# Macaron block on one core: queries of the second token group and the output signs held into the attention turns, the next element's first FFN begun in the prologue, small vectors loaded behind the matrices

## The chip, the core and the metric

One core of a Trainium2 chip. The metric is the device time of one execution in microseconds (us), as the median of several runs. The engines are TensorE (PE; PEld is its weight load), VectorE (DVE), ScalarE (ACT), GpSimd (POOL) and SyncE (SP, which here only issues DMAs).

## What is computed

Two batch elements of 1024 tokens, 512 wide, fp32. Cut to what matters:

```python
def bitnet_linear(x, weight, scale):            # q (512), k (128), v (128), o (512) outputs
    s = max(mean(abs(weight), axis=1), 1e-8)
    y = (x @ sign(weight / s).T) * (s * scale)
    return nan_to_num(y, nan=0, posinf=1e6, neginf=-1e6)

def attn(x):                                    # 32 heads of 16, 8 key/value heads
    q, k, v = (bitnet_linear(x, w, sc) for w, sc in ...)
    a = softmax(q @ k.T / sqrt(16))             # every head, 1024 x 1024
    return bitnet_linear(a @ v, o_weight, o_scale)

def ffn(x):                                     # base matrix + 8 experts of rank 16, top 2
    w = top2_softmax(x @ W_router.T)
    return x @ W_base.T + b_base + 2 * sum_e(w[e] * (x @ A[e].T) @ B[e].T)

x = x + 0.5 * ffn(layernorm(x))                 # first FFN
x = x + attn(layernorm(x))
x = x + 0.5 * ffn(layernorm(x))                 # second FFN
```

## The kernel before

Tokens are taken in groups `(b, g)`: batch element `b`, group `g` of 512 tokens (four tiles of 128). `first(b, g)` is the first FFN, the second layer norm and the projections of a group. Its projections come in six parts, items 0 to 3 for the queries (each serves two key/value heads' groups), 4 for the keys, 5 for the values. A part is eight fp32r matmuls (`pq`, L541; sign matrix times high and low half of the input) or 32 small ones (`pv`), a scaled copy `y` on ACT (L546), the replacement of NaN and infinities in `finite` (`lo`, `ma`, `z` on VectorE and GpSimd), a split of the result into a high and a low half (L574 on ACT, L580), and four stores to DRAM. For element 0 the query parts that are not marked `fast` store from the ACT and the GpSimd queue (L577, L584), all others from SP. `second(b, g)` normalises the attention output, applies the output projection (`po`, L679) and runs the second FFN (names ending in `s`, as `pbs`, `phs`, where the first FFN has `pbf`, `phf`). In an FFN `pt` are transposes, `ph` the router and low-rank matmuls (L363), `hwp` transposes of the weighted low-rank part, `pb` the base matmuls in fp32 (L388 and L393), and the bias is added on GpSimd (L383).

`binarize` makes the signs and scales of a weight matrix: absolute values on ACT, their sums by fp32 matmuls with ones (`pm_k`, `pm_q`, `pm_v`, `pm_o`, L488), reciprocals `rs` on VectorE (L498), products on GpSimd (L502), signs on ACT (L506, L509).

Attention is cut into 32 units: element, half of the queries (512), key/value head. A unit takes four turns. In a turn the scores of one unit are computed for the row maxima (`m`, eight matmuls, L796, reduced by eight VectorE instructions `mn`, L804), those of the unit before for the exponentials (`e`, 16 matmuls, L831 and L835, with eight ACT instructions `es`, L838), and the exponentials are multiplied with the values (`av`, L868). The first turns have no exponentials yet (lead-in). `place` loads a unit's queries and keys from DRAM; unit 8 is the first that needs queries of token group 1 of element 0, unit 16 the first of element 1.

The order of instructions on every engine is made while the program is built. Work is written as generators (strands) that yield the engine they want next: `"P"` TensorE, `"v"` VectorE, `"a"` ACT, `"g"` GpSimd, `"d"` SP, `"u"` a condition, `"r"` a buffer, `"j"` a join. `Flow` gives places to strands by rank (a lower number goes first) and by an estimate of when a result is due. Before the loop (the prologue) `flow.play` runs the strands freely. In `attention` three written orders say where in a turn a strand may place an instruction: `F` on TensorE, `V` and `W` on VectorE, `C` and `D` on ACT. A turn is `LEAD_IN` as long as there are no exponentials, else `FULL` when a strand wants TensorE (with places `F`), else `BARE`. `need` and `until` place everything that is left until a condition holds. At most three chains of strands are alive at a time; a chain starts at the turn that stands beside it in `chains`.

In `ffn_tiles`, `early` says that the base matmuls of all tiles are begun ahead of the routing. It is `flow.free`, true in the prologue and behind the loop.

Of the kernel before, what the change touches and what calls it, by code (L numbers as in the profile page):

```python
# [12 lines left out]
ALU = mybir.AluOpType  # L13
AX = mybir.AxisListType

P = 128
# [9 lines left out]
TG = 4  # L26
# [6 lines left out]
def macaron_kernel(ctx: ExitStack, tc: tile.TileContext, x_in, wbT, b_base, wrT, aT, bT,  # L33
                   wqT, q_sc, wkT, k_sc, wvT, v_sc, woT, o_sc, out):
    nc = tc.nc
# [39 lines left out]
    bh = const.tile([P, D], F32, name="bh")  # L75
    nc.gpsimd.dma_start(bh, b_base.partition_broadcast(P))
    wraw = {}
# [11 lines left out]
    qsc = const.tile([P, KC], F32, name="qsc")  # L89
    nc.gpsimd.dma_start(qsc, q_sc)  # L90
    ksc = const.tile([P, 1], F32, name="ksc")
    nc.gpsimd.dma_start(ksc, k_sc)
    vsc = const.tile([P, P], F32, name="vsc")
    nc.gpsimd.dma_start(vsc, v_sc.partition_broadcast(P))
    osc = const.tile([P, D], F32, name="osc")
    nc.gpsimd.dma_start(osc, o_sc.partition_broadcast(P))

# [37 lines left out]
    class Flow:  # L135
        def __init__(self):
            self.t, self.free, self.after, self.strands, self.n = 0, True, False, [], 0
            self.stock = dict(m=3, n=4, t=11, xT=2, xL=2, hT=1, fb=6)
            self.lock = None
            self.busy = dict.fromkeys("Pvagd", 0)  # L140
            self.pool = 0
# [199 lines left out]
    def ffn_tiles(xt, name, rank, tiles, xT, hT, mv, given, mv2, summed, store, loads):  # L341
# [36 lines left out]
        def base(t):  # L378
            if not early:
                yield "r", dict(t=1)  # L380
            yield "u", lambda: "bias" in signs
            yield "g", ""
            nc.gpsimd.tensor_tensor(xt[:, t, :], xt[:, t, :], bh, ALU.add)  # L383
            for c in range(KC):
                yield ("P", "P") if c else ("P", "", flow.t, 1)
                if c == 0:
                    pb = bank(f"pb{n}_{t}")
                nc.tensor.matmul(pb, xT[:, c, t * P:(t + 1) * P], wb[:, c, :],  # L388
                                 start=(c == 0), stop=False)
                flow.lock = bs[t] if c < KC - 1 else None  # L390
            yield "u", lambda: ready
            yield "P", "a", ready[0]
            nc.tensor.matmul(pb, hT[0][:, t * P:(t + 1) * P], lb, start=False, stop=True)  # L393
            if flow.free:
                yield "v", "P"
                nc.vector.scalar_tensor_tensor(xt[:, t, :], pb, 0.5, xt[:, t, :], ALU.mult, ALU.add)
                flow.give(fb=1, **({} if early else dict(t=1)))
            else:
                yield "a", "P"
                hb = t512(f"hb{n}_{t}")  # L400
                nc.scalar.activation(hb, pb, AF.Copy, scale=0.5)  # L401
                flow.give(fb=1)
                yield "g", "a"
                nc.gpsimd.tensor_tensor(xt[:, t, :], xt[:, t, :], hb, ALU.add)  # L404
                if not early:
                    flow.give(t=1)
            if store is not None:
                yield ("a" if flow.free else "d"), "v" if flow.free else "g"
                (nc.scalar if flow.free else nc.sync).dma_start(store[t * P:(t + 1) * P, :],
                                                                xt[:, t, :])  # L410
            if mv2 is not None:
                yield "v", "v" if flow.free else "g"
                stats(xt, t, mv2, n)
                summed.add(t)


        bs, ready, early = {}, [], flow.free
        if early:
# [60 lines left out]
    def binarize(w, n_out, name, sc, rank, at):  # L479
# [29 lines left out]
        nc.scalar.activation(wr[:, KC - 1, :], w[:, KC - 1, :], AF.Sign)  # L509

        if name in "vo":
            yield "v", ""
            nc.vector.tensor_tensor(sc, s, sc, ALU.mult)
        else:
            yield "P", "", None, 1
            pt = bank(f"col_{name}")
            for c in range(n_out // P):
                nc.tensor.transpose(pt[:, c * P:(c + 1) * P], s[:, c * P:(c + 1) * P], ident)
            yield "v", "P"
            nc.vector.tensor_tensor(sc, sc, pt[:, 0:n_out].rearrange("p (c n) -> p c n", n=P)[:, :, 0],  # L520
                                    ALU.mult)
            flow.give(fb=1)
# [70 lines left out]

    def qkv(b, g, xs, items, ranks, fast):

        at = ("v", flow.t)
        for i, rank in zip(items, ranks):
            parts[b, g, i] = [None]
            yield "u", lambda: ("q" if i < KC else "k" if i == KC else "v") in signs
            parts[b, g, i][0] = flow.spawn(qkv_part(b, g, xs, i, fast.get(i, 0), at), rank)  # L600
# [63 lines left out]
    def o_proj(b, g, hs, rank, mv, given, fast=False):  # L664
# [39 lines left out]
        for t in range(TG):  # L704
# [14 lines left out]
            "A3 m0(3) e0(0) V e0(5) D e1(0) e0(7) e0(6) e1(5) m0(2) e1(7) V e1(6) W m0(5) m0(4)")  # L719
    LEAD_IN = ("m0(0) m0(6) m0(1) V m0(7) F C S V m0(4) m0(2) V F C m0(5) V F C V m0(3) V F C V")  # L720
    FULL, BARE, LEAD_IN = (
# [156 lines left out]

    def attention(chains, n0):

# [3 lines left out]
        flow.stock["fb"] -= 4  # L884
        live = []

# [14 lines left out]
        for n in range(n0, TU * len(units) + LEAD + 1):  # L901
            begin = flow.t = max(flow.t, begin + span)
            m, e, a = todo(n, 0), todo(n, LEAD), todo(n, LEAD + 1)
            live = [c for c in live if not c.done]
# [58 lines left out]

    def first(b, g, items, ranks, fast={}, loads=None):

# [9 lines left out]
        else:  # L975
# [5 lines left out]
              for t, c in ((tag, bufs), ("xL", 2))]  # L981
        yield "j", [flow.spawn(ln_T(xt, f"a{b}_{g}", mv2, summed, t, xs, rank), rank)
                    for t in (((0, 1), (2, 3)) if split else (range(TG),))]
        yield from qkv(b, g, xs, items, ranks, fast)

# [18 lines left out]
    def usec(t):  # L1004
        return int(t / 0.115)

    def later_constants():
        yield "v", "", usec(12)
        nc.vector.tensor_scalar(bh, bh, 0.5, None, ALU.mult)
        signs["bias"] = bh  # L1010
        yield "g", "", usec(14), 4
        nc.gpsimd.memset(two_r.bitcast(F32), 0.0)
# [7 lines left out]

    def chain_o():
        yield from binarize(wraw["o"], D, "o", osc, 8, usec(36))
        yield "d", "x"
        yield "d", "x"
        load_x(1, 1)
# [4 lines left out]
    with tc.manual_schedule():  # L1030
# [3 lines left out]
        flow.spawn(binarize(wraw["q"], D, "q", qsc, 2, usec(24)), 2)  # L1034
        flow.spawn(first(0, 1, (4, 5, 0, 1, 2, 3), (3, 5, 6, 6, 6, 6), {4: 2}, [usec(14 + t) for t in range(TG)]), 3)
        flow.spawn(binarize(wraw["v"], P, "v", vsc, 4, usec(24)), 4)
        flow.spawn(chain_o(), 5.5)
        early = flow.spawn(begin(), 5)
        flow.play(lambda: early.done)
        t0 = flow.t  # L1040
        flow.play(lambda: flow.t > t0 + usec(3))
        T1 = TU * NQB * G
        QL = (15, 16)
        chains = [(0, lambda g=g: first(1, g, (4, 5, 0, 1, 2, 3), (10 + g,) * 3 + (15 + g,) * 3))
                  for g in range(NG)]
        for k, (b, g) in enumerate(((0, 0), (0, 1), (1, 0))):
# [4 lines left out]
        chains.append((TU * ((B * NQB - 1) * G + 4) + LEAD + 2, lambda: final(1, 1, hs)))  # L1051
        attention(chains, TU // 2)
        for c in chains:
# [42 lines left out]
```

## Time and profile before

| | us |
|---|---|
| median of 3 runs | 1160.17 (1158.27 to 1160.95) |
| profiled execution | 1160.11 |
| its span, first to last instruction | 1157.1 |
| TensorE busy | 1067.0 (92%) |
| VectorE busy | 882.9 (76%) |
| ScalarE busy | 669.5 (58%) |
| GpSimd busy | 296.0 (26%) |
| mean granted TensorE clock | 0.975 |

The prologue reaches to the start of the loop near 122 us (turn 2; the first 16 score matmuls of turns 0 and 1 are placed ahead of it by `begin`), the loop's last scores stand near 1050 us, the last exponential near 1082 us, and the second FFN of element 1 follows. Times of rows are microseconds from the span's start; a row of the timeline names engine, line, operation, tiles and count, and in brackets how long the engine was idle before it and what ended that. A busy TensorE is not one at its peak.

### The profile page before, as it was taken

To read this page: it belongs to the slowest core of one execution; us is meant where nothing else is said; L and a number is where in the kernel's file an instruction comes from. 1 tells how busy PE (TensorE), PEld (TensorE's weight loads), DVE (VectorE), ACT (ScalarE), POOL (GpSimd) and SP (SyncE) were. 2 spreads that over 40 slices of the span, in tenths; PEclk is the share of its full clock that TensorE was granted. 3 is DMA by queue.
4 is the path that set the end of the run, shared out by engine and by line. 5 is a ranking of instruction groups with operands and counts; after the bars stand their busy time and mean duration, and the time that the engine had idled before them with its cause. 6 is when DMAs were issued, how large, how long until landed. Compare 5 with 4: busy or idle time off the path is not lost.

```text
span 1157.1 us, 21521 instructions
## 1 busy us (share of the span) xinstructions
PE 1067.0 (92%) x8453; PEld 592.0 (51%) x8453; DVE 882.9 (76%) x1694; ACT 669.5 (58%) x1309; POOL 296.0 (26%) x351
## 2 busy tenths in 40 slices
PE   6888779999999999999979899999999999999968
PEld 4546345554455554454645455544445555444543
DVE  5677997877787787788788897797778879874372
ACT  2312258766577566567556678566667866566620
POOL 5233743001010041022254232141111314321270
PEclk9989689999999999999999999999999999999979
DMA  8023543211111124223244241211123420311101
GB/s 275 1 85 98 133 160 83 47 47 47 47 47 47 47 84 120 47 67 94 94 123 138 66 127 32 65 43 49 49 64 100 117 45 24 85 57 51 42 20 54
DMA packets 48797, 87.43 MB, mean 76 GB/s; under 512 B 9768, under 2 KB 12840, under 8 KB 48696
## 3 DMA queue, kind: packets, MB, share of 16 engines
q1 hardware_dynamic: 42552, 74.45, 22.8%
q10 hardware_dynamic: 3872, 7.34, 1.9%
q0 software_dynamic: 2272, 4.27, 1.5%
q8 instruction: 66, 1.08, 0.4%
q14 instruction: 35, 0.29, 0.1%
HBM read 51.19 MB, written 34.32 MB: 74 GB/s over the span
## 4 chain that ended last, share of the span: by engine, by line
PE 70%; DVE 20%; ACT 3%; DMA 2%; issue 2%; POOL 1%; SPq 0%; ACTq 0%; POOLq 0%; DVEq 0%
PE av L868 19%; PE m L796 15%; DVE mn L804 10%; PE e L831 9%; PE e L835 7%; PE pbs L388 5%; PE pbf L388 5%; ACT es L838 2%; PE po L679 2%; PE pq L541 2%; PE pbf L393 1%; PE phf L363 1%; PE phs L363 1%; PE pv L558 1%; DMA arw<-in_wrT 1%
## 5 line engine op out<-in xcount | busy, mean ns | idle before, releaser
L804 DVE TENSOR_REDUCE mn<-m 128x1 f32<-128x512 f32 x1024 | 648.0, 681 | 157.8 <-PE e L835 79.6
L838 ACT ACTIVATE es<-e 128x512 f32<-128x512 f32 x1024 | 542.1, 603 | 300.6 <-PE e L835 265.8
L796 PE MATMUL m<-k 64*128 64x512 f32 x1024 | 366.1, 443 | 21.1 <-DVE mn L804 12.3
L868 PE MATMUL av<-es,vaug 128*32 128x256 f32 x4096 | 275.3, 386 | 20.0 <-ACT es L838 10.4
L831 PE MATMUL e<-k 64*128 64x512 f32 x1024 | 276.7, 441 | 0.2
L796 PEld LDWEIGHTS m<-k 64*128 64x128 f32 x1024 | 170.3, 187 | 168.7 <-DVE mn L804 83.3
L835 PE MATMUL e<-mq,two_r 64*128 64x512 f32 x1024 | 253.2, 396 | 1.9 <-DMA mq<-mT 1.9
L868 PEld LDWEIGHTS av<-es,vaug 128*32 128x32 f32 x4096 | 108.0, 109 | 148.3 <-issue 81.3
L831 PEld LDWEIGHTS e<-k 64*128 64x128 f32 x1024 | 121.0, 186 | 58.8 <-DVE mn L804 29.5
L835 PEld LDWEIGHTS e<-mq,two_r 64*128 64x128 f32 x1024 | 143.3, 186 | 14.4 <-issue 2.4
L388 PE MATMUL pbf<-wb,xTf 128*128 128x512 f32 x128 | 61.2, 605 | 0.0
L388 PE MATMUL pbs<-wb,xTs 128*128 128x512 f32 x128 | 60.7, 605 | 0.0
L404 POOL TENSOR_TENSOR x<-x,hbf 128x512 f32<-128x512 f32 x8 | 10.3, 1283 | 161.8 <-ACT hbf L401 161.8
L383 POOL TENSOR_TENSOR x<-x,bh 128x512 f32<-128x512 f32 x32 | 41.2, 1311 | 3.2 <-ACT xns L306 3.1
L388 PEld LDWEIGHTS pbs<-wb,xTs 128*128 128x128 f32 x128 | 22.7, 189 | 26.2 <-issue 25.7
L580 POOL TENSOR_TENSOR z<-z,y 128x512 fp32r<-128x512 f32 x17 | 22.9, 1345 | 51.2 <-ACT y L574 51.1
L388 PEld LDWEIGHTS pbf<-wb,xTf 128*128 128x128 f32 x128 | 22.7, 189 | 25.7 <-issue 24.9
L265 POOL TENSOR_TENSOR ro<-ro,loo 128x512 f32<-128x512 f32 x16 | 20.7, 1292 | 58.7 <-DVE ro L263 51.0
L260 POOL TENSOR_SCALAR loa<-y 128x512 f32<-128x512 f32 x17 | 11.5, 676 | 85.1 <-ACT y L546 84.2
L404 POOL TENSOR_TENSOR x<-x,hbs 128x512 f32<-128x512 f32 x8 | 10.3, 1285 | 88.7 <-ACT hbs L401 88.7
L697 POOL TENSOR_TENSOR x<-x,ro 128x512 f32<-128x512 f32 x16 | 20.5, 1280 | 46.7 <-DVE ro L269 42.4
L631 POOL TENSOR_TENSOR an<-an,rb 128x512 f32<-128x512 f32 x15 | 19.7, 1317 | 48.9 <-DMA rb<-rd 48.6
(205 smaller groups left out, 1029.2 us busy)
## 6 DMA issues: line engine op xcount, KB each, us to landing
k<-qd SPq DMA_DIRECT2D x32, 512.0 KB
k<-kd SPq DMA_DIRECT2D x62, 256.0 KB
ad<-avs SPq DMA_DIRECT2D x32, 256.0 KB
qd<-y SPq DMA_DIRECT2D x18, 256.0 KB
qd<-z SPq DMA_DIRECT2D x18, 256.0 KB
an<-ad SPq DMA_DIRECT2D x15, 256.0 KB
rb<-rd SPq DMA_DIRECT2D x15, 256.0 KB
x<-in_x SPq DMA_DIRECT2D x14, 256.0 KB
```

The source lines that it names most:

```text
L363: nc.tensor.matmul(ph[:, i, 0:ER + E], xT[:, c, t * P:(t + 1) * P], arw[:, c, :], start=(c == 0), stop=(c == KC - 1))
L383: nc.gpsimd.tensor_tensor(xt[:, t, :], xt[:, t, :], bh, ALU.add)
L388: nc.tensor.matmul(pb, xT[:, c, t * P:(t + 1) * P], wb[:, c, :], start=(c == 0), stop=False)
L541: nc.tensor.matmul(pq, w_[:, k, :], xs[j][:, k, :], start=(k + j == 0), stop=(k + j == KC))
L580: (nc.vector if fast else nc.gpsimd).tensor_tensor(lo, o, y, ALU.subtract)
L679: nc.tensor.matmul(po, hs[j][:, c, t * P:(t + 1) * P], wo[:, c, :], start=(c + j == 0), stop=(c + j == KC))
L796: nc.tensor.matmul(s["m", i], s["q"][rows_of(h), h // 2, qt * P:(qt + 1) * P], s["k"][rows_of(h), kh * 512:(kh + 1) * 512], start=True, st ...
L804: nc.vector.tensor_reduce(s["mn"][:, 2 * (h % 2) + h // 2, qt, kh:kh + 1], s.pop(("m", i)), AX.X, ALU.max, negate=True)
L831: nc.tensor.matmul(t, s["k"][rows_of(h), kt * P:(kt + 1) * P], s["q"][rows_of(h), h // 2, :], start=True, stop=False)
L835: nc.tensor.matmul(t, two_r[rows_of(h), h // 2, :], s["mq"][rows_of(h), :], start=False, stop=True)
L838: nc.scalar.activation(e, s.pop(("e", i)), AF.Exp, scale=HD ** -0.5)
L868: nc.tensor.matmul(s["av"][32 * h:32 * h + 32, cols], s["v"][:, kt, :], s["es"][kt * REP + h][:, cols], start=(kt + half == 0), stop=(kt + ...
```

## The change

It does four things. The load of the bias and of the four scale vectors moves from the head of the program into `later_constants`, on GpSimd's queue behind the first reciprocal roots; the first FFN of group (0, 0) adds its bias after the base matmuls are placed instead of before them. The query parts of group (0, 1) wait until turn 8 (`hold`), and `chain_o`, the output signs and the load of the last `x` group behind them, until turn 10. `first(1, 0)` is started by `ahead` in the prologue, from 60 us of the planner's time, with rank 10 and without `early`, and is handed to the loop in `live`. `LEAD_IN` loses four of its seven `V` places.

```diff
     bh = const.tile([P, D], F32, name="bh")
-    nc.gpsimd.dma_start(bh, b_base.partition_broadcast(P))
...
-    nc.gpsimd.dma_start(qsc, q_sc)
-    nc.gpsimd.dma_start(ksc, k_sc)
-    nc.gpsimd.dma_start(vsc, v_sc.partition_broadcast(P))
-    nc.gpsimd.dma_start(osc, o_sc.partition_broadcast(P))
...
+            self.turn = 0
...
         def base(t):
             if not early:
                 yield "r", dict(t=1)
-            yield "u", lambda: "bias" in signs
-            yield "g", ""
-            nc.gpsimd.tensor_tensor(xt[:, t, :], xt[:, t, :], bh, ALU.add)
+                yield "g", ""
+                nc.gpsimd.tensor_tensor(xt[:, t, :], xt[:, t, :], bh, ALU.add)
             for c in range(KC):
...
+            if early:
+                yield "u", lambda: "bias" in signs
+                yield "g", ""
+                nc.gpsimd.tensor_tensor(xt[:, t, :], xt[:, t, :], bh, ALU.add)
             yield "u", lambda: ready
...
-            if flow.free:
+            if early or flow.free:
                 yield "v", "P"
                 nc.vector.scalar_tensor_tensor(xt[:, t, :], pb, 0.5, xt[:, t, :], ALU.mult, ALU.add)
...
-        bs, ready, early = {}, [], flow.free
+        bs, ready, early = {}, [], flow.free and (rank < 10 or flow.after)
...
+        yield "u", lambda: "scales" in signs
         if name in "vo":
...
-    def qkv(b, g, xs, items, ranks, fast):
+    def qkv(b, g, xs, items, ranks, fast, hold):
...
+            if i in hold:
+                yield "u", lambda: flow.turn >= hold[i]
...
-    LEAD_IN = ("m0(0) m0(6) m0(1) V m0(7) F C S V m0(4) m0(2) V F C m0(5) V F C V m0(3) V F C V")
+    LEAD_IN = ("m0(0) m0(6) m0(1) V m0(7) F C S m0(4) m0(2) V F C m0(5) F C V m0(3) F C")
...
-    def attention(chains, n0):
+    def attention(chains, n0, live):
...
+            flow.turn = n
...
     def later_constants():
-        yield "v", "", usec(12)
+        yield "g", "", usec(9), 7
+        nc.gpsimd.dma_start(bh, b_base.partition_broadcast(P))
+        yield "v", "", usec(18)
         nc.vector.tensor_scalar(bh, bh, 0.5, None, ALU.mult)
         signs["bias"] = bh
-        yield "g", "", usec(14), 4
+        for t, src in ((ksc, k_sc), (qsc, q_sc), (vsc, v_sc.partition_broadcast(P)),
+                       (osc, o_sc.partition_broadcast(P))):
+            yield "g", "", None, 5
+            nc.gpsimd.dma_start(t, src)
+        signs["scales"] = True
+        yield "g", "", None, 4
...
     def chain_o():
+        yield "u", lambda: flow.turn >= 10
         yield from binarize(wraw["o"], D, "o", osc, 8, usec(36))
...
-        flow.spawn(first(0, 1, (4, 5, 0, 1, 2, 3), (3, 5, 6, 6, 6, 6), {4: 2}, [usec(14 + t) for t in range(TG)]), 3)
+        flow.spawn(first(0, 1, (4, 5, 0, 1, 2, 3), (3, 5, 6, 6, 6, 6), {4: 2}, [usec(14 + t) for t in range(TG)],
+                         {0: 8}), 3)
...
+        def ahead():
+            yield "u", lambda: flow.t >= usec(60)
+            yield from first(1, 0, (4, 5, 0, 1, 2, 3), (10,) * 3 + (15,) * 3)
+        live = [flow.spawn(ahead(), 9)]
...
-        chains = [(0, lambda g=g: first(1, g, (4, 5, 0, 1, 2, 3), (10 + g,) * 3 + (15 + g,) * 3))
-                  for g in range(NG)]
+        chains = [(0, lambda: first(1, 1, (4, 5, 0, 1, 2, 3), (11,) * 3 + (16,) * 3))]
...
-        attention(chains, TU // 2)
+        attention(chains, TU // 2, live)
```

More of the change, by code (lines that the diff above doesn't have):

```diff
@@ L884, in attention @@
         flow.stock["fb"] -= 4
-        live = []
         def need(*keys):
@@ L962, in macaron_kernel, with first @@
     signs = {}
-    def first(b, g, items, ranks, fast={}, loads=None):
+    def first(b, g, items, ranks, fast={}, loads=None, hold={}):
         yield "u", lambda: (b, g) in xg
@@ L983, in first @@
                     for t in (((0, 1), (2, 3)) if split else (range(TG),))]
-        yield from qkv(b, g, xs, items, ranks, fast)
+        yield from qkv(b, g, xs, items, ranks, fast, hold)
     def second(b, g, rank, hs, split=False):
```

## The prediction

> **What bounds the kernel now.** First the page's slices of the span (40 of about 29 us each): busy tenths of TensorE and VectorE, and the clock that TensorE was granted.
>
> ```profile
> PE   6888779999999999999979899999999999999968
> DVE  5677997877787787788788897797778879874372
> PEclk9989689999999999999999999999999999999979
> ```
>
> From the seventh slice on TensorE is at 90% or more almost throughout, at full clock; matmuls bound that part, so work can be moved there but not hidden. In slices three to six (60 to 175 us) TensorE has room, the clock drops to 0.6, and VectorE is the one at 90%. A second view, busy time by window, cut at the turns of the attention loop (a turn begins with the first of its eight score matmuls `m`, L796). Columns: length, then PE, PEld, DVE, ACT, POOL busy, granted clock, DMA share, GB/s.
>
> ```profile
> 90.60:109.50 18.90, 17.87 (x103) 13.70 (x102) 13.88 (x27) 4.73 (x11) 4.90 (x8) 0.95 0.23 68
> 109.50:121.70 12.20, 9.96 (x40) 6.01 (x39) 12.20 (x17) 2.69 (x4) 10.32 (x10) 1.00 0.64 164
> 121.70:130.80 9.10, 5.66 (x14) 2.86 (x13) 9.10 (x13) 2.50 (x4) 5.97 (x8) 0.57 0.42 92
> 130.80:142.30 11.50, 8.90 (x19) 4.32 (x17) 11.36 (x22) 3.14 (x5) 9.53 (x10) 0.50 0.50 140
> 142.30:149.60 7.30, 3.85 (x12) 2.00 (x11) 7.30 (x14) 0.69 (x1) 4.92 (x8) 0.73 0.40 118
> 149.60:160.60 11.00, 7.65 (x42) 4.71 (x41) 10.91 (x20) 5.45 (x11) 6.74 (x8) 0.66 0.73 215
> ...
> 272.50:280.10 7.60, 7.60 (x63) 3.72 (x62) 5.72 (x10) 4.23 (x8) 0.00 (x0) 1.00 0.44 126
> ```
>
> These are turns 0 to 5, and turn 22 as a steady one. In turns 2 to 5 VectorE is busy for 38.7 of 38.9 us and TensorE runs at half clock; in turn 22 TensorE is busy all the time and VectorE has 1.9 us free. So the same vector work costs time in turns 2 to 5 and nothing in a turn like 22.
>
> The vector timeline names what stands there beside the row maxima, and the timelines of PE and ACT show three more waits:
>
> ```profile
> 124.84 2.55 DVE L498 RECIPROCAL rs_o<-s_o 128x128 f32<-128x128 f32 x3
> 127.32 1.85 DVE L262 TENSOR_SCALAR ma<-y 128x512 uint8<-128x512 f32 x1
> 144.23 1.49 DVE L263 TENSOR_SCALAR z<-y 128x512 f32<-128x512 f32 x1
> ```
> ```profile
> 14.97 6.71 PE L363 MATMUL phf<-arw,xTf 128*128 128x136 f32 x32 [2.50 <-DMA arw<-in_wrT]
> 66.05 0.66 PE L466 MATMUL hwpf<-ident,hwf 128*128 128x128 f32 x2 [4.64 <-DVE topf L428]
> ```
> ```profile
> 152.53 0.62 ACT L574 CAST y<-z 128x512 fp32r<-128x512 f32 x1 [9.49 <-DVE z L269]
> ```
>
> The first group is the output signs' reciprocals and the second group's queries, whose operations take 1.5 to 2 us beside GpSimd work where the same L263 takes 0.41 without it. Last, the chain of waits at the change of batch element:
>
> ```profile
> 584.30 6.02 DMA kd<-z
> ...
> 590.95 4.16 DMA k<-kd
> ```
>
> **The change, part by part.** The sum is made against the profiled execution: span 1157.1 us, 3.0 us around it, 1160.1 in all (the median is 1160.17). I read what moves from the order in which the two built kernels' instructions stand, and price it with rows of this trace.
>
> *Small vectors behind the matrices.* Five GpSimd DMAs (two of 256 KB, one of 64 KB, two tiny) leave the first 4 us. In the first 14 us DMA moved 4.06 MB, 0.59 of it theirs: at about 370 GB/s, 1.6 us. What waits is TensorE for `arw`, 2.50 us; but the last copy of `xTf` ends only at 13.1, so at most 14.97 - 13.1 = 1.9 us goes unless `x` also lands earlier. I take -1.9 (0 to -3). The DMAs come back behind two bias additions on POOL's queue; the issues took 0.56 to 0.82 us there, the landings up to 10.2, and the scales are first used near 50 us, so this is free.
>
> *The next element's first FFN in the prologue, up to 90.6 us.* VectorE gets four BN statistics with aggregates (0.69 + 0.18) and four normalisations of 0.5; less 2.4 us in which it idled, and other small shifts, its work in front of the first row maximum grows by 3.3 us. Against it: `pq` of query 0 (3.4 us) and a `pbf` now stand in front of the `hwp` transpose and fill its 4.64 us wait, and the bias additions on POOL no longer stand beside the routing operations of VectorE (0.55, 1.22, 0.92, 1.12 us there, 0.15 to 0.16 each elsewhere: 3.2 us). I take -1 (-4 to +3.3).
>
> *Turns 0 and 1.* `pm_o` (eight fp32 matmuls, 3.4 us), five half-parts of queries and 4 us of vector work go; transposes and `phf` of the new FFN come. VectorE's work by median durations goes from 25.6 to 23.7: I take -2 (0 to -4).
>
> *Turns 2 to 5.* The four `V` places that the lead-in order loses only choose which vector work stands there; what is left is counted. VectorE's work goes from 28.6 to 22.0 us by median durations; the real time of before was 38.9, 1.36 times its 28.6. Scaled alike 22.0 gives 30, with nothing but the work itself 22, and TensorE needs about 25 (8 x 0.23 for scores a turn, 4.3 for one `pbf` tile in turn 4, 7.3 for turn 5, now a full one). I take 29, or -10 (-5 to -15). The clock bears on this end: with less TensorE work in the lead-in, turns 2 to 4 may stay near the 0.50 granted at 130 to 142 us, where a `pq` matmul starts every 0.43 us instead of 0.23. Turn 4's 6.1 us of TensorE work would then be 12.2, and the gain 5 us smaller; that is the -5.
>
> The Trainium skill speaks against the change here: "TensorE: Matmul & The Clock Gate", Part 1, says that the array falls to half rate after an idle window of about 3.4 us and recovers after a busy one. By that rule turn 4's `pbf` would lose some 1.7 us before the clock returns, an estimate from the page, and the gain be 8.3 instead of 10.
>
> *The turns that take the work.* TensorE's side work in turns 6 to 126, by start-to-start times (`pb` 0.43 a matmul, `pq` and `po` 0.23 to 0.25, `pv` 0.116, `ph` 0.128, transposes 0.11), is 142.5 us before and 143.5 after: what comes (four queries, `pm_o`) weighs what goes (one FFN's transposes, `ph` and first tile). The kinds of turns change. Mean time without side work, by kind and successor: full before full 5.85, full before bare 7.79, bare before bare 6.17, bare before full 5.11. Before has 66, 17, 20 and 18 of them, after 75, 11, 25 and 10:
> 876.4 - 142.5 = 733.9 becomes 729.9; with the side work -3.0. The stretch 563.4 to 595.2 (turns 62 and 63) takes 8.1 us more than its kinds; its chain runs from the key part of group 1 through the store and load above. In the new order that part (1.12) and half the values (1.86) stand a turn earlier: -3.0. Against this, four query parts with two ACT-issued stores each (0.6 us) now stand among exponentials: 4.8 us, of which ACT's slack (3.4 of 7.6 us in turn 22) should hide over half: +2 (0 to +22, see the rivals). The DMAs of the fifth `x` load move back too, on SP, behind loads that have a whole unit's time. Together -4.
>
> *The end.* Three `pbs` matmul pairs (2.6 us) no longer spill past turn 126, and most of the last-but-one group's transposes and `phs` (5.4 us of TensorE) now stand in turns without scores, where TensorE was busy 21.7 of 25 us (1059 to 1084) with ACT at 20.9; half of that fits. I take -5 (0 to -9).
>
> Sum: -1.9 - 1 - 2 - 10 - 4 - 5 = -24, so 1160.1 - 24 = **1136 us**.
>
> **Rivals.** *Only the lead-in gives* (0.22). Half clock keeps turns 2 to 5 at -5, the start and end give -3 in place of -9.9 with turns 0 and 1, the turns nothing: 1152. For it: TensorE's total work is the same, and 1067 of 1157 us are already busy. Against: full turns that follow each other are the cheapest in the table.
>
> *ACT stalls in the turns* (0.10), slower. ACT takes its queue in order; the copy L574 of a held query waits for VectorE's `z`, and all exponentials behind it wait too, then the `av` matmuls. The place is turns 7 to 13, where before this copy stood in the lead-in and waited 9.49 us with hardly an exponential behind it. Price: 9.49 less the 1 us that ACT waits for `e` anyway, 8.5 for each of four parts, 34 against my 2: 1136 + 32 = 1168. It decides from 6.5 us a part (26 us for four). Turn 5, with one such copy, took 11.0 against about 5.5, so 5.5 has been seen. Against it: turns 39 to 41 and 51 to 53 hold the same parts of the next element and took 7.35 to 7.84.
>
> *The loads don't arrive earlier*: then `arw` still ends the wait near 15 us, +1.9, 1138; inside my range.
>
> **How the numbers follow.** The forecast has 0.68. Its own terms reach 1121 when the lead-in gives 15, the end 9 and the start 6 and a little is lost to ACT; upward the partial case at 1152 is taken in, and the slow case alone is left out, with a few in a hundred below. Range 1121 to 1152. A difference of 0.2% (2.3 us) is about what a measurement of this kernel can tell. Faster by more: 0.68 + nearly all of 0.22, 0.88; within it 0.02; slower 0.10.
>
> **What would show it.** Right: `phf` starts near 13 us with no wait for `arw`; the `hwp` wait at 66 us is gone; the stretch of turns 2 to 5 takes 27 to 32 us with VectorE still near 100%; turns 7 to 13 take 7.3 to 8 each; eleven changes from full to bare; the last `es` ends near 1063. Wrong: turns 7 to 13 at 9 us or more with ACT waiting at L574, a turn 4 of 12 us at clock 0.5, or a first row maximum later than 93 us.

## The result and the profile after

The changed kernel takes 1175.26 us (1173.67 to 1175.99), against 1160.56 for the kernel before on the same chip: ratio 1.0123, 95% interval [1.0104, 1.0141]. It is slower; 1136 was forecast, and 1121 to 1152 as the range. Of the profiled executions, the span went from 1157.1 to 1174.2 us.

Cut at the same places as in the prediction (a turn starts with the first of its eight `m` matmuls, now L798), the two spans divide like this:

| stage, us | before | after | forecast | measured |
|---|---|---|---|---|
| up to turn 0 | 90.6 | 83.6 | -2.9 | -7.0 |
| turns 0 and 1 | 31.1 | 29.7 | -2 | -1.4 |
| turns 2 to 5 | 38.9 | 41.5 | -10 | +2.6 |
| turns 6 to 126 | 885.8 | 907.3 | -4 | +21.5 |
| turn 127 to the end | 110.7 | 112.1 | -5 | +1.4 |

The start gained more than forecast, the end and the lead-in gave nothing, and the turns that take the work lost 21.5 us. The page's slices of the span after:

```profile
PE   6869699998999979999979899999999999989868
DVE  6878767788878876777888697779987877795352
PEclk9989599999999989999989999999999999999979
```

In the same view of before, the clock was at 0.6 in slice five and full from the seventh slice on. Now slice five is at 0.5, and the fifteenth (411 to 440 us) has TensorE at 0.7 and the clock at 0.8: a hole in a part that was full before. Busy time by window for turns 0 to 5 and for the turn in that hole; columns: length, then PE, PEld, DVE, ACT, POOL busy, granted clock, DMA share, GB/s.

```profile
83.60:105.10 21.50, 21.09 (x130) 17.79 (x130) 15.10 (x28) 7.09 (x15) 3.62 (x4) 0.88 0.15 49
105.10:113.30 8.20, 7.75 (x50) 5.98 (x49) 7.70 (x10) 1.99 (x3) 7.05 (x7) 1.00 0.60 157
113.30:122.50 9.20, 3.62 (x10) 1.79 (x9) 6.40 (x23) 2.04 (x6) 7.06 (x8) 0.66 0.73 164
122.50:135.00 12.50, 6.37 (x13) 2.95 (x12) 12.33 (x21) 0.21 (x1) 6.54 (x8) 0.50 0.43 134
135.00:148.20 13.20, 13.20 (x20) 4.71 (x19) 7.54 (x15) 0.58 (x1) 0.00 (x0) 0.55 0.36 82
148.20:154.70 6.50, 6.50 (x29) 3.13 (x28) 4.97 (x8) 4.51 (x9) 1.28 (x1) 1.00 0.00 0
...
433.70:447.70 14.00, 10.56 (x63) 4.58 (x62) 7.76 (x15) 5.36 (x11) 0.00 (x0) 0.76 0.67 177
```

Turn 4 (135.0 to 148.2) is TensorE alone: busy 13.20 of 13.20 us at 0.55 of the clock, with VectorE idle for 5.7. It is the "turn 4 of 12 us at clock 0.5" that the prediction named as a sign against it. Turn 5 is as short as hoped. Turn 43 (433.7) took 14 us where a full turn takes 7.6.

The timeline of the changed kernel, all engines, in order of time, with the rows that answer the prediction's:

```profile
12.56 4.51 PE L359 MATMUL phf<-arw,xTf 128*128 128x136 f32 x32
60.62 0.41 PE L465 MATMUL hwpf<-ident,hwf 128*128 128x128 f32 x2 [1.66 <-DVE topf L427]
83.56 1.50 PE L798 MATMUL m<-k 64*128 64x512 f32 x4 [7.20 <-DMA k<-kd]
119.75 0.73 DVE L265 COPY_PREDICATED z<-ma,y 128x512 f32<-128x512 uint8 x1 [2.66 <-POOL z L261]
124.00 4.92 POOL L378 TENSOR_TENSOR x<-x,bh 128x512 f32<-128x512 f32 x4
124.72 4.24 DVE L438 CAST idff<-idxf 128x8 f32<-128x8 uint32 x1
429.72 1.20 SPq L619 DMA_DIRECT2D rs<-ad  x1
434.53 0.35 DVE L625 RECIPROCAL rs<-rs 128x32 f32<-128x32 f32 x1 [1.87 <-DMA rs<-ad]
437.45 0.35 DVE L625 RECIPROCAL rs<-rs 128x32 f32<-128x32 f32 x1 [2.02 <-DMA rs<-ad]
1105.04 0.41 PE L465 MATMUL hwps<-ident,hws 128*128 128x128 f32 x2 [4.23 <-DVE hws L456]
1105.28 5.29 PE L383 MATMUL pbs<-wb,xTs 128*128 128x512 f32 x8
```

`phf` starts at 12.56 without a wait and runs in 4.51 us instead of 6.71; the `hwp` wait is 1.66 instead of 4.64; TensorE is then done so early that it waits 7.20 us for the first keys. In turn 2 VectorE waits 2.66 us for a `z` of GpSimd. In turn 3 a conversion of 128x8 numbers holds VectorE for 4.24 us while GpSimd adds four bias tiles. In turn 43 VectorE stands before two reciprocals until softmax sums arrive from DRAM. At the end TensorE waits 4.23 us for the routing of the last-but-one FFN, and its first base tile then runs at half clock (5.29 us for what otherwise takes 3.60). The chain of waits, longest pieces, shows two DMAs inside the loop that were not among them before:

```profile
432.20 5.23 DMA rs<-ad
...
642.97 5.81 DMA k<-kd
```

What the 21.5 us of turns 6 to 126 consist of can be counted from the trace of all 121 turns. TensorE's idle time went from 34.8 to 42.9 us. Half clock while TensorE was busy (one minus the granted clock, times the busy time) went from 1.7 to 12.7. That is 8.1 + 11.0 = 19.1; what is left, TensorE's work counted at full clock, is 2.4. The half clock stands in six stretches: five follow a wait of TensorE of 1 us or more, the one in turn 58 none above 0.3. This is an account of where the time went; what caused it is asked below.

### The profile page after: what moved, and what is told of

It reads as the page before. It is cut to its first block, busy times and chain, and to the rows that moved or that the text cites. A ratio compares the mean times of both kernels' runs of the same rounds, so it can differ in the third digit from the quotient of the medians.

```text
span 1174.2 us, 21503 instructions
## 1 busy us (share of the span) xinstructions
PE 1077.1 (92%) x8453; PEld 592.5 (50%) x8453; DVE 884.7 (75%) x1698; ACT 665.4 (57%) x1305; POOL 297.0 (25%) x349
## 4 chain that ended last, share of the span: by engine, by line
PE 70%; DVE 20%; issue 3%; POOL 2%; ACT 2%; DMA 2%; SPq 1%; ACTq 0%; DVEq 0%; POOLq 0%
PE av L870 18%; PE m L798 15%; PE e L833 9%; DVE mn L806 9%; PE e L837 7%; PE pbs L383 5%; PE pbf L383 3%; PE pq L541 2%; PE po L681 2%; PE phs L359 1%; PE pbs L392 1%; ACT es L840 1%; PE pv L558 1%; DVE stf L270 1%; DMA k<-kd 1%
## 5 line engine op out<-in xcount | busy, mean ns | idle before, releaser
L798 PE MATMUL m<-k 64*128 64x512 f32 x1024 | 372.6, 447 | 40.1 <-DVE mn L806 22.1
L870 PE MATMUL av<-es,vaug 128*32 128x256 f32 x4096 | 278.2, 390 | 16.7 <-issue 9.5
L798 PEld LDWEIGHTS m<-k 64*128 64x128 f32 x1024 | 171.7, 189 | 194.5 <-DVE mn L806 99.5
L837 PE MATMUL e<-mq,two_r 64*128 64x512 f32 x1024 | 256.2, 399 | 0.0
L383 PE MATMUL pbf<-wb,xTf 128*128 128x512 f32 x128 | 64.8, 635 | 0.0
L383 PEld LDWEIGHTS pbf<-wb,xTf 128*128 128x128 f32 x128 | 23.3, 197 | 26.5 <-issue 24.2
L261 POOL TENSOR_TENSOR z<-z,loa 128x512 f32<-128x512 f32 x17 | 23.2, 1366 | 32.8 <-DVE z L259 27.5
```

The costliest lines, as they stand in the source:

```text
L261: nc.gpsimd.tensor_tensor(o, o, lo_, ALU.add)
L798: nc.tensor.matmul(s["m", i], s["q"][rows_of(h), h // 2, qt * P:(qt + 1) * P], s["k"][rows_of(h), kh * 512:(kh + 1) * 512], start=True, st ...
L837: nc.tensor.matmul(t, two_r[rows_of(h), h // 2, :], s["mq"][rows_of(h), :], start=False, stop=True)
L870: nc.tensor.matmul(s["av"][32 * h:32 * h + 32, cols], s["v"][:, kt, :], s["es"][kt * REP + h][:, cols], start=(kt + half == 0), stop=(kt + ...
```

## The experiments

The theory after the result, A: the loss lies in single waits, each in a place of its own and each followed by half clock. The rival B: TensorE is full in the turns, so the held work costs there what it saves elsewhere, and a wait that is removed comes back as another.

**Parts.** Four kernels divide the change.

E1: before, with the loads of the small vectors moved and the bias behind the base matmuls. This order holds in every FFN that is `early`, not in group (0, 0) alone: in both groups of the prologue and in the two FFNs behind the loop.

> Before with the first part of the change alone: bias and scale vectors loaded behind the matrices, the first group's bias added after its base matmuls. In the changed kernel's profile the first base matmuls started 4.6 us earlier than before, where the forecast gave 1.9. Theory A (this part is sound and its gain reaches the end): the first row maximum at 86 us, total 1155.5. Rival B (the gain is eaten by the waits for the keys and in the lead-in, which VectorE bounds): first row maximum within 1 us of before, total 1160.

1144.14 us, ratio 0.9872 [0.9846, 0.9899]: far more than either theory gave. The first row maximum's matmul stands at 79.7 instead of 90.6, and the end is 4.6 us shorter.

E2: the changed kernel without the early start.

```diff
-        live = [flow.spawn(ahead(), 9)]
+        live = []
-        chains = [(0, lambda: first(1, 1, ...))]
+        chains = [(0, lambda g=g: first(1, g, ...)) for g in range(NG)]
```

> The changed kernel without the early start of the next element's first FFN; queries and output signs still held. Theory A (the loss is in single waits in the turns, followed by half clock, where side work of the next element meets its due time): the FFN now begins only at turn 5, so everything of the last group that is due at unit 16 is forced into turn 62 (32 projection steps instead of 12); turns 2 to 5 fall to about 26 us, turns 62 and 63 grow from 32 to 45 us, total 1172. Rival B (TensorE is full in the turns, and the held work simply costs there what it saves in the lead-in): turns 2 to 5 26 us, total about 1160.

1159.21 us, ratio 0.9982 [0.9970, 0.9994]. Turns 62 and 63 took 48.8 us, as A said; but turns 0 and 1 fell to 20.2 and turns 2 to 5 only to 33.4, and the total is B's. The holds do empty the lead-in (turns 0 to 5: 53.6 us, 70.0 before); the early start fills it again (71.2 in the changed kernel).

E3: the changed kernel without the two holds. E4: with the queries held, the output signs not.

```diff
 E3, E4
     def chain_o():
-        yield "u", lambda: flow.turn >= 10
 E3 alone
-        ... [usec(14 + t) for t in range(TG)], {0: 8}), 3)
+        ... [usec(14 + t) for t in range(TG)]), 3)
```

> The changed kernel without the two holds (queries of group 1 and output signs are placed as early as they can be); early start and late loads stay. Theory A: the last x group is loaded in the lead-in again, so the last group's projections stand in turns 55 to 60, nothing is forced into turn 62 and the stop at unit 16 (8 to 10 us) goes; turns 2 to 5 stay near 40 us or grow to 45; total 1154. Rival B (the early start is what hurts, by bunching the side work into full turns): as slow as the changed kernel, 1172 to 1178.

1149.61 us, ratio 0.9910 [0.9889, 0.9930]. Turns 62 and 63 take 11.4 us instead of 32.1: the stop at unit 16 is gone, as A said, and B's 1172 to 1178 is out.

> The changed kernel with only the queries held, not the output signs. Theory A: x of the last group comes early, so the last group's query parts stand in turns 58 to 62 and the stop at unit 16 shrinks; turns 2 to 5 shorter than in the kernel without holds (about 32 us); total 1150. Rival B (holding query parts into full turns costs as much as it saves): 1158 or more, with turns 8 to 14 at 9 us or more.

1158.32 us, ratio 0.9973 [0.9956, 0.9990]. Turns 8 to 14 took 7.3 to 8.7 us, so there is no stall in them; yet turns 6 to 126 are 11.3 us longer than in E3, with half clock under a busy TensorE and idle time the same or less (5.0 and 29.0 us against 4.9 and 30.7). That is B's price: the query parts' 32 matmuls are 7.4 us of TensorE time (0.23 each), put where it has none to spare; what makes up the rest of the 11.3 is not shown. With E1, E3 and E4, the change can be added up part by part (spans, us):

| added to the row above | span | up to turn 0 | turns 0-5 | 6-126 | from 127 |
|---|---|---|---|---|---|
| before | 1157.1 | 90.6 | 70.0 | 885.8 | 110.7 |
| late loads, order of the bias (E1) | 1141.7 | -10.9 | -0.2 | +0.3 | -4.6 |
| early start, lead-in order (E3) | 1147.7 | +3.4 | +3.2 | -7.6 | +7.0 |
| queries held (E4) | 1155.8 | -0.2 | -2.6 | +11.3 | -0.4 |
| output signs held (after) | 1174.2 | +0.7 | +0.8 | +17.5 | -0.6 |

The shares depend on the order of adding. E2 gives another one: on top of E1, the holds without the early start add 18.2 us (-16.2 in turns 0 to 5, +26.7 in 6 to 126, +7.1 from 127), the early start on top of them 14.3. So the early start alone costs 6.0, the holds alone 18.2, both together 32.5: 8.3 us come from their meeting. The end is 7 us longer with either of the two.

**E10: late loads without the order of the bias.** E1 with the bias added in front of the base matmuls again:

```diff
         def base(t):
+            yield "u", lambda: "bias" in signs
+            yield "g", ""
+            nc.gpsimd.tensor_tensor(xt[:, t, :], xt[:, t, :], bh, ALU.add)
             for c in range(KC):
...
-            if early:
-                yield "u", lambda: "bias" in signs
-                yield "g", ""
-                nc.gpsimd.tensor_tensor(xt[:, t, :], xt[:, t, :], bh, ALU.add)
```

> Before with only the loads of the bias and the scales moved; the first group's bias is added in front of its base matmuls, as before. This and the run with the order of the bias as well (1144) share out that run's 16 us. Theory A (each half has its own place: the loads make the first base matmuls 4 us earlier, the order of the bias keeps GpSimd off the routing and lets the tail's bases start): 1155. Rival B (the early loads are the whole of it): 1146.

1159.49 us, ratio 0.9996 [0.9981, 1.0011]: nothing. Timelines, first before, then E1, then E10:

```profile
12.15 4.93 POOL L383 TENSOR_TENSOR x<-x,bh 128x512 f32<-128x512 f32 x4
21.52 3.60 PE L388 MATMUL pbf<-wb,xTf 128*128 128x512 f32 x8
```
```profile
16.07 3.60 PE L383 MATMUL pbf<-wb,xTf 128*128 128x512 f32 x8
58.23 0.41 PE L465 MATMUL hwpf<-ident,hwf 128*128 128x128 f32 x2 [1.88 <-DVE topf L427]
```
```profile
25.20 4.94 POOL L379 TENSOR_TENSOR x<-x,bh 128x512 f32<-128x512 f32 x4 [6.94 <-DVE bh L1011]
26.75 4.12 PE L384 MATMUL pbf<-wb,xTf 128*128 128x512 f32 x8
68.12 0.44 PE L462 MATMUL hwpf<-ident,hwf 128*128 128x128 f32 x2 [4.16 <-DVE hwf L453]
```

Before, the first group's bias was added by 17.1 us and held nothing: the base matmuls stood at 21.52, right behind `phf`. With late loads alone, the bias that comes late holds them until 26.75; with the additions behind them they start at 16.07. The second group's `hwp` wait is still 4.16 us in E10 (4.64 before) and 1.88 in E1, and the end takes 110.5 us in E10, 106.1 in E1. So late loads alone are worth nothing, and all 15 us need the order of the bias. Whether that order alone, with early loads, would give a part of them was not run.

**Single waits.** E5: reciprocals planned later. E6: unit 17's load a turn earlier.

```diff
 E5
-        first = flow.t
+        first = flow.t + usec(6)
 E6
-            if m and m[0] + 1 < len(units) and m[1] == 2:
+            if m and m[0] + 1 < len(units) and m[1] == (1 if m[0] + 1 == 17 else 2):
```

> The changed kernel with one number added: the reciprocals of the softmax sums are planned 6 us later after their load is issued. In the changed kernel turn 43 took 13.96 us, because four reciprocals stand in VectorE's queue and wait for sums whose loads SP issues behind sixteen query stores; the row maxima behind them wait too, and the clock falls to 0.76. Theory A (such single waits make the loss): turn 43 falls to about 8 us, total 1175.3 - 5.5 = 1169.8. Rival B (TensorE is full, another wait takes its place): less than 1.5 us less.

1177.73 us, ratio 1.0147 [1.0123, 1.0171]: no gain. Turn 43 still took 13.89 us, and this stands at its end (timeline of E5):

```profile
445.80 0.76 PE L798 MATMUL m<-k 64*128 64x512 f32 x1 [6.10 <-DMA k<-kd]
```

The wait went from the reciprocals to the next unit's keys. B was right here.

> The changed kernel with the queries and keys of unit 17 loaded one turn earlier. Before turn 68 TensorE waited 3.08 us for its keys, whose loads SP issued behind query stores, and then ran at 0.75 of the clock. Theory A: this wait and the half clock behind it go, turns 67 and 68 together fall from 17.9 to about 13.5 us, total 1171. Rival B: less than 1.5 us, since the stores that are now behind the load make something else late.

1173.91 us, ratio 1.0106 [1.0081, 1.0132]. Turn 67 fell from 11.46 to 10.38 only; TensorE still waited 1.96 us for these keys, although SP had issued their load by 639.5 and TensorE stood until 646.6. Here an earlier issue did not help; the transfers themselves are late.

E9: the query stores of element 1 on the ACT and GpSimd queues.

```diff
-            own = b == 0 and i < KC and not fast
+            own = i < KC and not fast
```

> The changed kernel with the query parts of element 1 stored from the ACT and GpSimd queues, as those of element 0 are, instead of all from SP. The two experiments on turns 43 and 67 showed that a later reciprocal or an earlier load only moves the wait: in both the loads of keys landed 8 us or more after their issue, behind up to sixteen stores of 256 KB. Theory C (the loads stand behind the stores in one DMA queue): with other queues for the stores the wait in turn 43 and the one before turn 68 go, turn 43 about 8 us and turn 67 about 8, together -8, less 2 for ACT's issues, total 1169. Rival D (the DMA engines are shared and it is bandwidth that is short): both waits stay, total 1175 or more.

Turn 43 by window, in E9:

```profile
432.10:439.80 7.70, 7.70 (x63) 3.52 (x62) 5.59 (x11) 5.42 (x11) 3.62 (x3) 1.00 0.68 190
```

The wait is gone: 7.7 us at full clock, with DMA as busy as before (0.68, 190 GB/s against 0.67, 177). So C holds at the place in this form: the loads stood behind the stores on SP. What E9 does not tell apart is the DMA queue and SP's own order. In the changed kernel SP issued nine query stores of 256 KB from 419.30 on and the first `rs` load only at 429.72; in E9, without these stores, it issued that load at 417.40. For a late transfer speaks E6: its last key load was issued at 638.86, behind twelve stores, and took 7.59 us to land, against 4.16 in before and 4.47 in the changed kernel's start. But DMA was busy for 0.88 of that time, so D is not out there. The Trainium skill, "DMA: Bandwidth & Descriptors", section "Queues, rings and completion order", says that each DMA engine takes the descriptors of one queue in order and goes round between queues; E5, E6 and E9 fit this, and none of them shows it apart from SP's order.

The total is 1175.37, ratio 1.0150 [1.0122, 1.0177]: no gain. In the profiled execution, the fastest of four (1171.6 to 1179.6), turns 6 to 126 are only 4.2 us shorter than in the changed kernel, since turns 35, 38, 63 to 65 and 70 each grew by 0.9 to 3.3 us.

E7: the bias of group (1, 0) behind each tile's base matmuls.

```diff
+            if not early and rank != 10:
                 yield "g", ""
...
-            if early:
+            if early or rank == 10:
                 yield "u", lambda: "bias" in signs
```

> The changed kernel with the bias of group (1, 0) added after each tile's base matmuls instead of four additions at a time in front of them. In the changed kernel's turn 3 a 128x8 conversion on VectorE took 4.24 us beside these four additions on GpSimd. Theory A (the four additions hold VectorE, and TensorE stops and stays at half clock through turns 3 and 4): the conversion takes 0.2 us, turns 2 to 5 fall from 41.5 to about 33 us, total 1167. Rival B (VectorE had this work to do anyway, the half clock of turns 2 to 4 comes from too little TensorE work): turns 2 to 5 fall by no more than the 4 us of the conversion, total 1171.

1172.11 us, ratio 1.0101 [1.0079, 1.0123]. Beside a single addition of 1.27 us the conversion took 0.72, turn 3 fell from 12.5 to 9.0, turn 4 to 11.9, turns 2 to 5 to 36.6: 4.9 us less, near rival B; in the total, its interval overlaps that of the changed kernel. VectorE's conversion, then the windows of turns 3 and 4 in E7:

```profile
124.61 0.72 DVE L439 CAST idff<-idxf 128x8 f32<-128x8 uint32 x1
```
```profile
122.30:131.30 9.00, 6.43 (x13) 2.99 (x12) 8.81 (x21) 0.21 (x1) 2.91 (x6) 0.50 0.64 188
131.30:143.20 11.90, 11.90 (x20) 4.28 (x19) 7.57 (x15) 0.58 (x1) 0.00 (x0) 0.62 0.36 91
```

The hold-up by GpSimd cost 3.5 us in its turn; the half clock of turn 4 stays without it.

E8: the second FFN of group (1, 0) held until turn 130.

```diff
         yield from o_proj(b, g, hs, rank, mv, given, fast)
+        if (b, g) == (1, 0):
+            yield "u", lambda: flow.turn >= 130
         yield from ffn(xg[b, g], f"s{b}_{g}", rank, ...)
```

> The changed kernel with the second FFN of group (1, 0) held until turn 130, so that its base matmuls are again begun ahead of its routing. In the changed kernel this FFN began in turns 127 to 132, its base matmuls were put behind the routing, and after the last av TensorE waited 4.23 us for VectorE and ran the first base tile at half clock (5.3 us instead of 3.6). From turn 127 to the end it took 112.1 us, the kernel with the late loads alone 106.1. Theory A (the order of this FFN is the loss at the end): the tail falls to about 106.5, total 1169.5. Rival B (the end is set by the last group's output projection, which can't start earlier): within 1.5 us of the changed kernel.

1164.75 us, ratio 1.0033 [1.0017, 1.0048]. From turn 127 to the end 101.7 us instead of 112.1, and every turn before within 0.7 us of the changed kernel: 10.4 us, more than A gave. Timeline of E8:

```profile
1102.78 3.60 PE L383 MATMUL pbs<-wb,xTs 128*128 128x512 f32 x8
1106.21 0.38 PE L465 MATMUL hwps<-ident,hws 128*128 128x128 f32 x2
```

A base tile now stands in front of `hwps`, TensorE does not wait for the routing, and the tile runs at full clock. In E2, without the early start, the wait is there as in the changed kernel (timeline of E2):

```profile
1089.61 0.66 PE L465 MATMUL hwps<-ident,hws 128*128 128x128 f32 x2 [4.24 <-DVE hws L456]
```

**What the hold of the output signs costs.** E13: E4, with the load of the last `x` group alone delayed.

```diff
+        yield "u", lambda: flow.turn >= 21
         yield "d", "x"
         load_x(1, 1)
```

> The kernel with only the queries held (1158 us, turns 6 to 126 889.8 us), with the load of the last x group alone delayed to turn 21, about where the changed kernel issues it; the output signs stay in the lead-in. Theory A (the hold of the output signs costs because the load behind them makes the last group's work late, bunched and due at unit 16): turns 62 and 63 grow from 12.8 to about 28 us, turns 6 to 126 to 900 to 907, total 1170 or more. Rival B (the output signs' work itself is what costs in the turns): no change, 1158.

1162.15 us, ratio 1.0033 [1.0009, 1.0056]; 1170 is out. Turns 62 and 63 did grow, from 12.8 to 25.3 us, but turns 6 to 61 gave back 12.0, since the same work no longer stood there. Turns 6 to 126 are 893.4: the late load explains 3.6 of the 17.5 us. From there to the changed kernel (907.3) half clock under a busy TensorE grows by 7.7 and idle time by 7.1 us, mostly in turns 20, 40, 41, 43, 58 and 63. In E6, which issues the same instructions up to turn 64, turns 20, 40 and 58 came out 0.9 to 1.5 us shorter, so part of it moves from run to run; which placement makes each of these waits stays open.

**Lead-in.** E14: E7 with two extra matmuls into an unused bank behind each score matmul of turns 2 and 3. E15: the same in the combined kernel below.

```diff
+WARM = 2
...
                         m_tile(m[0], m[1] * 2 * REP + i)
+                        for _ in range(WARM if order is LEAD_IN and n < n0 + 2 else 0):
+                            nc.tensor.matmul(warm, signs["k"][:, 0, :], signs["q"][:, 0, :],
+                                             start=True, stop=True)
```

> The run with the bias of group (1, 0) after its base matmuls (1172), with two extra 128x512 matmuls into an unused bank behind each of the 16 score matmuls of turns 2 and 3: work that serves nothing. Theory A (turns 2 to 5 are bound by the half clock, which stays as long as TensorE has gaps): turns 3 and 4 run near full clock, turn 4 falls from 11.9 to about 8 us, turns 2 to 5 from 36.7 to 32, total 1167. Rival B (VectorE's work bounds them, or the extra matmuls delay the scores): turns 2 to 5 stay at 36 or grow to 40, total 1172 to 1176.

1177.59 us, ratio 1.0156 [1.0125, 1.0186]; turns 2 to 5 grew to 46.7. Timeline and windows (turns 3 and 4) of E14:

```profile
121.15 0.50 PE L800 MATMUL m<-k 64*128 64x512 f32 x1 [0.97 <-DVE mn L808]
```
```profile
122.70:138.50 15.80, 15.80 (x29) 7.15 (x28) 10.32 (x24) 0.17 (x1) 2.23 (x4) 0.50 0.30 91
138.50:152.70 14.20, 14.20 (x22) 4.89 (x21) 5.71 (x10) 0.59 (x1) 0.00 (x0) 0.51 0.31 75
```

TensorE stood for 0.97 us, the clock fell, and it stayed at half for 30 us in which TensorE, by the profile, was busy without a gap.

> The combined kernel (1137) with the same extra matmuls. Its turns 2 to 5 took 38.8 us at clocks of 0.71, 0.50, 0.73 and 0.62. Theory A: turns 2 to 5 fall to about 35, total 1133. Rival B: 1137 to 1141.

1138.24 us, ratio 0.9794 [0.9765, 0.9823]. Here the same matmuls kept the clock at 1.00 through turns 2 to 4; turns 2 to 5 took 39.3 us (38.8 without them), because the extra work itself then filled TensorE (busy for all 24.2 us of turns 2 to 4, for 18.1 of as many without it). Whether filler can pay is left open.

E16: the changed kernel with the old lead-in order.

> The changed kernel with the lead-in's old order (seven V places instead of three). The prediction held that these places only choose which vector work stands there: then turns 2 to 5 stay within 2 us of 41.5. Theory A (they decide how much of the new FFN's routing, and so of its base matmuls, falls into the half-clock turns): turns 2 to 5 change by 4 us or more; seven base matmuls in place of five stand there at about 1 us for each half instead of 0.43, so they grow to 46. The last group is due later still (44 steps forced into turn 62 instead of 20), which costs another 10 us or more: total 1188.

1175.72 us, ratio 1.0139 [1.0118, 1.0159]. Turns 2 to 5 40.7 us, so the four places decide little in total, as the prediction had it. Of use is turn 4 (window of E16):

```profile
138.40:145.80 7.40, 7.40 (x22) 2.64 (x21) 5.43 (x10) 0.60 (x1) 1.52 (x3) 1.00 0.19 40
```

It holds the same eight scores and five base steps as the changed kernel's turn 4, and takes 7.4 us at full clock against 13.2 at 0.55: half clock cost that turn 5.8 us.

**Combined.** E11: the changed kernel with E3's, E7's and E8's edits. E12: E11 with E9's edit. E17: E11 with the old lead-in order.

> The changed kernel without the two holds, with the bias of group (1, 0) after its base matmuls and with the second FFN of group (1, 0) held until turn 130. If the single effects add up: 1149.6 without the holds, less 10.4 at the end, less 3 in turns 2 to 5 gives 1136. Theory A (the effects are in separate places): 1136 to 1139. Rival B (TensorE is full, the effects take each other's place): about the 1144 of the late loads alone.

> The same with the query stores of element 1 on the ACT and GpSimd queues. In the kernel without holds turn 67 took 9.4 us behind a key load that landed late. Theory C: that turn falls to about 6, total 3 us under the run before, 1133 to 1136. Rival D: no gain, or a loss of up to 3 us, since ACT issues stores between exponentials.

> The combined kernel (1137) with the old lead-in order. No base matmuls stand in its turns 2 to 4 either way, so by theory A and by the prediction alike the difference is small: 1134 to 1140.

E11 takes 1137.07 us, ratio 0.9812 [0.9790, 0.9833], and E17 1135.93, 0.9793 [0.9774, 0.9813]; the two can't be told apart. Both beat the kernel before and the changed one. The single effects added up to 1136, so A holds for these. E12 takes 1143.48, 0.9861 [0.9838, 0.9884]: turn 67 fell from 9.0 to 5.0 us, and turns 6 to 126 as a whole grew by 8.1. Other queues for the stores mend their place and cost more elsewhere.

## Why the prediction was wrong

*Up to turn 0* (-2.9, measured -7.0): right in sign, too small. Late loads and the order of the bias give -10.9 together (E1), in two places. The first base matmuls stand 5.45 us earlier: the wait for `arw` goes, as priced, and `phf` itself runs in 3.87 us instead of 6.71, for which the sum had no term; why it ran longer before is open. The other 5.4 us stand around the second group's `hwp` wait (4.64 us before, 1.88 in E1) and the half clock behind it. The prediction had named that wait and the bias additions beside the routing, but set them off against the early start's vector work. The early start takes 3.4 us back (E3), at the bound of +3.3 named for it, not at the value taken. (The 4.06 MB read there were moved in 16 us, not 14; the 1.6 us priced from them do not change.)

*Turns 0 and 1* (-2, measured -1.4): right, and by the work that was named: +3.1 us with what comes (E3), -3.9 when the output signs go.

*Turns 2 to 5* (-10, measured +2.6): the step that failed is the scaling of VectorE's work, 22.0 us at the old ratio of 1.36. VectorE did not bound turn 4: half clock did, 5.8 us (E16), and turn 3 held a GpSimd stop of 3.5 us (E7) that the sum didn't have, although the prediction had priced just such additions beside routing operations in the start (3.2 us). Nor did VectorE's own work bound turn 2 (busy 6.40 of 9.20 us): it waited 2.66 us for GpSimd, which stood with query stores and additions, and TensorE stood for 4.12. The 25 us that TensorE was said to need don't follow from the terms listed, which give 17 to 19; the four turns hold 19.4 at full clock. The clock was named, but as an end of the range at 5 us, and it came together with the stop. The rule weighed there, the Trainium skill's "TensorE: Matmul & The Clock Gate", Part 1, would have taken 1.7 us off the gain; turn 4 alone lost 5.8, and E14's 30 us at half clock with a busy TensorE disagree with its recovery after a busy window of about 3.4 us. The measurement decides.

*The turns that take the work* (-4, measured +21.5): the failed step is that side work was summed as busy time, and kinds of turns by their means from before, where half clock was 1.7 us in 121 turns. That sum itself was off by about 6 us (+2.4 is what is left beside idle time and half clock, -4 was taken); it starts from 876.4 us where the trace has 885.8 for these turns, without saying what it leaves out, but this falls out of the difference. What it had no term for is that moved work changes what meets: the stores of query parts with the sums and keys of other units on SP (turn 43, 6.3 us, E9), and half clock, 11.0 us in all, more than the 8.1 us that the waits themselves grew by. The note that loads on SP "have a whole unit's time" was about the wrong transfers. The stretch of turns 62 and 63 did not lose 3 us either (32.1 against 31.8); the vector work of the parts forced into turn 62 stands in its chain, as `ma`, `z`, `vd` and `ro` from 594 to 610 us.

*The end* (-5, measured +1.4): E1 gave -4.6 for a reason not in the prediction (the base matmuls of the last groups no longer wait for the bias; 110.5 us in E10), and the early start +7.0. The failed step is that transposes and `phs` in turns without scores would be time won. The FFN that began there lost its early base matmuls, `early` being false inside the loop, and E8 shows 10.4 us for that. It is not the early start as such: in E2, without it, that FFN begins inside the loop too, and the end takes 113.2 us.

*The rivals.* The slower one, ACT stalls at L574 in turns 7 to 13, is not what happened: those turns took 7.22 to 8.02 us, as the forecast said. Its total (1168) is near the result by another mechanism. Of the signs listed, `phf`, the first row maximum, turns 7 to 13 and the eleven changes from full to bare came out right, the `hwp` wait in the main (1.66 us of 4.64 are left); turns 2 to 5 and the last `es` (1098.8 instead of 1063) did not.

## What to carry to other kernels

Work moved out of a stretch with idle TensorE into one that is full costs its whole length there (the held queries: -2.6 in the lead-in, +11.3 in the turns), and the stretch it left is only shorter if nothing refills it. When steps move, list the transfers that each issues and what else uses that queue within the next 20 us: a late load there stops the engines, and the clock charges as much again. An edit with several parts is best priced and tried part by part: here one part was worth -15 us and the others gave it back twice, 8.3 us of it only because they met.

## What the runs showed of the hardware

A wait of 1 to 3 us on TensorE can cost more afterwards than it lasts: after 0.97 us the clock stayed at 0.50 for 30 us of unbroken matmuls (E14), while the same filler in another kernel kept it at 1.00 (E15); what decides between the two is open. A VectorE operation of 128x8 that takes 0.72 us beside one GpSimd addition took 4.24 beside four in a row (E7, changed kernel): it ended with the series, at 129.0. Key loads that elsewhere landed 4.2 to 4.5 us after their issue took 7.6 to 9.2 behind query stores on SP (8.97 in E5, 7.59 and 9.22 in E6). The wait in turn 43 went when the stores took other queues, at the same DMA throughput (E9); the loads were then also issued 12 us earlier.
